# A decoder layer with 16 experts: a quarter of the dense expert moved to the start of the expert loop, the closing additions on one engine

## The chip, the cores and the metric

The kernel runs on one core of a Trainium2 chip. The metric is device time of one execution, in microseconds (us); lower is better. A core has five engines with an instruction queue each: TensorE (PE; its weight loads are counted apart as PEld), VectorE (DVE), ScalarE (ACT), GpSimd (POOL) and SyncE (SP). SP, ACT and POOL also issue DMA transfers here; a row marked SPq or ACTq is such an issue. Each queue runs in its order; the engines wait for each other by semaphores.

## The reference, cut to what matters

`x` is 16 x 64 tokens of 256 values, 1024 tokens in all. After self attention and cross attention comes a mixture of experts with a residual:

```python
scores = softmax(xt @ Wg.T)                      # 16 experts
# the two best of four groups of experts, and in them the four best experts
weights = take_along_axis(scores, topi, axis=1)
h = silu(xt @ W1[e].T) * (xt @ W3[e].T)          # 176 hidden values per expert
y = sum over e of combine[:, e] * (h @ W2[e].T)
z = silu(xt @ Ws1.T) * (xt @ Ws3.T) @ Ws2.T      # shared expert
x = x + y + z
```

## The kernel before, in words

**Work and tiles.** The 1024 tokens are eight tiles of 128 (`NI` = 8), `x[0]` to `x[7]`, which lie two by two in `x_pairs`. Products are made from two float parts of each operand, a rounded high part and the rest: `parts_of` (L111 to L113) rounds on ScalarE (L112) and subtracts on VectorE (L113), and `matmuls` (L102 to L105) sums three products of parts. The attention comes first, up to about 450 us; the experts are the rest.

**Fifteen experts by slots.** For experts 0 to 14 the rows of tokens are sorted into slots: GpSimd scatters them to `xd` in HBM, with 384 slots for each expert. For each expert:

- `expert_weights` loads the weights by SP (L277), ScalarE makes their high part (`w<-w`, L278), and VectorE or GpSimd the low part (L283).
- `expert_inputs` loads the slots' rows (`xr`, by SP), turns them over on TensorE (six transposes, L1265) and makes their parts `xs` (L112, L113).
- `expert_hidden` does the up products (18 matmuls, L104), the silu on ScalarE (`g`, L1283, and `g2`, L1286), the products `h` and `h2` on VectorE (L1284, L1287), and their parts `hp` (L112, L113).
- `send_outputs` does the down products (three blocks of five matmuls, `av<-w,hp`), copies each block to `y` (L1299, ScalarE, or VectorE for one block of most experts), and GpSimd scatters `y` to `yd` in HBM (L1304, three scatters per expert), sorted by choice: a token's four experts are its choices 0 to 3, in the order in which their experts are done.

**The dense expert.** Expert 15 is computed for every token, with a weight that is zero where a token did not choose it; its weights `w_last` are in SBUF from early on. The tokens' first half is done before the loop (`dense_up`, `dense_gated`, `dense_out`). The second half is done in two quarters of 256 tokens: `dense_hidden` (18 up matmuls of 128 columns by 256, `mm<-xn,w_last`, then silu, product and parts) and `dense_output` (two blocks of five matmuls, `av<-w_last,hp`, each followed by `add_last`, L950 to L954, one VectorE addition L952 of the weighted result to `x`).

**The expert loop** (`for e in range(E + 1)`) is staggered: in step `e` the inputs of expert `e` are made, the hidden values of expert `e - 1`, and the outputs of expert `e - 2`. The hidden values of experts 0 and 1 stand at the head of steps 1 and 2. `weights_of_choices(1)`, in step 1, makes the weights of the second half's tokens; its exponential has an ACT table load of its own (L878), and the next silu another (L1283). In the last step the first quarter's hidden values are made (`h_p`).

**The tail.** After the scatters of experts 11 to 14, `load_outputs(k)` reads back choice `k` from `yd` in four transfers of 256 KB (`got<-yd`, L1320, all by SP; nine `got` buffers). `add_outputs(k)` adds them to `x`: two of three tiles by one VectorE instruction (L1334), the third by ScalarE, which scales (L1331), and GpSimd, which adds (L1332). The dense quarters stand between: choice 0, output of the first quarter, choice 1, hidden values and output of the second quarter, choices 2 and 3. Then eight transfers write `out`, by SP and ScalarE in turn (L1392).

**What sets the order.** A scheduler orders each engine's queue by a simulated timeline, bound by what the kernel writes out: inside `with tc.issue_after(i)` nothing is issued before `i`. `up_done[0]` is the last up matmul of the expert done last, `gated[0]` its last part, `silus[-1]` its last silu, `lows[-1]` the last part of the inputs. The tail stands behind the last scatters and `gated[0]`.

Of the kernel before, what the change touches and what calls it, by code (L numbers as in the profile page):

```python
# [29 lines left out]
AF = mybir.ActivationFunctionType  # L30
ALU = mybir.AluOpType
# [11 lines left out]
E, INTER, NGRP, TOPK, TOPKG = 16, 176, 4, 4, 2  # L43
# [28 lines left out]
def decoder_layer(ctx: ExitStack, tc: tile.TileContext, a: dict, out: bass.AP):  # L72
    nc = tc.nc
# [43 lines left out]
    x = [t[:, i, :] for t in x_pairs for i in range(2)]  # L117
# [168 lines left out]
    def expert_up(w, xs, n):  # L286


        ps = [mm_tile(cols=n) for _ in range(3)]
        return ps, [expert_up_part(k, w, xs, t) for k, t in enumerate(ps)][-1]  # L290
# [24 lines left out]
    with ExitStack() as attn:  # L315
# [643 lines left out]
        with (  # L959
# [109 lines left out]
            def dense_weights():  # L1069

                parts = [
                    xw.tile([128, 2, 2, 4 * HQ], F32R, tag=f"w_q{n}", name=f"w_last{n}")
                    .rearrange("p a b c -> p (a b c)")[:, :W_COLS]
                    for n in range(2)
                ]
                up = xb.tile([128, 3, 2, 2, DC], F32, tag="w_s", name="w_last_up")
                down = xb.tile([128, 2, D], F32, tag="w_o0", name="w_last_down")
                for t, cols in (
                    (up.rearrange("p a b c d -> p (a b c d)"), slice(0, W_UP)),
                    (down.rearrange("p a b -> p (a b)"), slice(W_UP, W_COLS)),  # L1080
                ):
                    nc.sync.dma_start(out=t, in_=a["W123"][E - 1][:, cols])
                    parts_of(t, parts[0][:, cols], parts[1][:, cols])
                return parts
# [18 lines left out]
            def dense_gated(g, up, g2, up2):  # L1103
                h_p = [
                    xa.tile([128, 512], F32R, tag=f"roped1{n}", name=f"dense1{n}", bufs=1)
                    for n in range(2)
                ]
                h_p.append(xa.tile([128, 512], F32R, tag="q_r", name="dense2"))
                nc.vector.tensor_tensor(g, up, g, ALU.mult)
                parts_of(g, h_p[0], h_p[1])  # L1110
                nc.vector.tensor_tensor(g2[:64], up2[64:], g2[64:], ALU.mult)
                parts_of(g2[:64], h_p[2][:64], h_p[2][64:])
                return h_p
# [15 lines left out]
            for n in range(len(units) + 2):  # L1129
# [58 lines left out]
                if n == 8:  # L1188
                    w_last = dense_weights()
                    with after(exps[-1]):  # L1190
                        routed.append(weights_of_choices(0))
                if n == 9:
# [30 lines left out]
                    with after(aimed, placed):  # L1223
# [4 lines left out]
                        h_p = dense_gated(*dense_ups)  # L1228
# [9 lines left out]
    gated, up_done = [None], [None]  # L1238
# [34 lines left out]
    def expert_hidden(w, xs, n):  # L1273


        ps, up_done[0] = expert_up(w, xs, n)
        g, h, g2, h2 = (
            fh.tile([128, SLOTS], F32, tag=tag, name=tag)[:, :n] for tag in ("g", "h", "g2", "h2")
        )
        h_p = [  # L1280
            fh.tile([128, SLOTS], F32R, tag=tag, name=tag)[:, :n] for tag in ("hp0", "hp1", "hp2")
        ]
        nc.scalar.activation(g, ps[0], AF.Silu)  # L1283
        nc.vector.tensor_tensor(h, ps[1], g, ALU.mult)  # L1284
        parts_of(h, h_p[0], h_p[1])
        silus.append(nc.scalar.activation(g2[64:], ps[2][:64], AF.Silu).ins)  # L1286
        nc.vector.tensor_tensor(h2[:64], ps[2][64:], g2[64:], ALU.mult)  # L1287
        gated[0] = parts_of(h2[:64], h_p[2][:64], h_p[2][64:])
        return h_p
# [24 lines left out]
    def load_outputs(k):  # L1314

        tiles = []
        for n in range(NI // 2):
            t = fy.tile([128, 2, D], F32, tag="got", name="got", bufs=9)
            first = (E - 1) * SLOTS + (TOPK - 1 - k) * NT + n * 256
            got = nc.sync.dma_start(  # L1320
                out=t, in_=yd[first : first + 256].rearrange("(i p) d -> p i d", p=128)
            ).ins
            behind(got, returned)
            tiles.append(t)
        return tiles

    def add_outputs(k, got, cw):
        for i in range(NI):
            y, w = got[i // 2][:, i % 2], cw[i // 4][:, k, i % 4 : i % 4 + 1]
            if i % 3 == 2:  # L1330
                nc.scalar.activation(y, y, AF.Copy, scale=w)  # L1331
                nc.gpsimd.tensor_tensor(x[i], x[i], y, ALU.add)  # L1332
            else:
                nc.vector.scalar_tensor_tensor(x[i], y, w, x[i], ALU.mult, ALU.add)  # L1334

    def dense_hidden(w, half, n):
        return expert_hidden(w, [p[:, :, n * 256 : n * 256 + 256] for p in normed[half]], 256)

    def dense_output(w, h_p, half, n, add):
        for b in range(2):  # L1340
            ps = av_tile()[:, :D]
            expert_output(ps, w, h_p, slice(b * 128, b * 128 + 128))
            add(half, 2 * n + b, ps)
# [6 lines left out]
    ws, xs, hs, got = {}, {}, {}, {}  # L1350
    with tc.issue_after(lows[-1]), tc.issue_after(silus[-1]):
        ws[0] = expert_weights(a["W123"][0], nc.vector)
    for e in range(E + 1):
        if e in (1, 2):

            low = lows[-1]
            hs[e - 1] = expert_hidden(ws[e - 1], xs[e - 1][0], SLOTS)
        if e < E - 1:
            low = lows[-1]
            with tc.issue_after(up_done[0] if e in (1, 2) else low):  # L1360
                xs[e] = expert_inputs(e)
            if e >= 1:
                with tc.issue_after(low), tc.issue_after(silus[-1]):
                    ws[e] = expert_weights(a["W123"][e], nc.vector if e < 3 else nc.gpsimd)
        if e == 1:
            with tc.issue_after(gated[0]), tc.issue_after(silus[-1]):
                routed.append(weights_of_choices(1))
        if 0 <= e - 1 < E - 1 and e > 2:
            hs[e - 1] = expert_hidden(ws[e - 1], xs[e - 1][0], SLOTS)
        if e - 2 >= 0:  # L1370
            if e == E:

                with tc.issue_after(gated[0]):
                    h_p = dense_hidden(w_last, 1, 0)
            last = send_outputs(e - 2, ws.pop(e - 2), hs.pop(e - 2), xs.pop(e - 2)[1])
            if e - 2 == E - TOPK - 2:
                short = slots_are_short()
            k = e - 2 - (E - 1 - TOPK)
            if k >= 0:
                got[k] = load_outputs(k)  # L1380
    with ExitStack() as behind_last:
        for ins in (*last, gated[0]):
            behind_last.enter_context(tc.issue_after(ins))
        cw = [r[0] for r in routed]
        add_outputs(0, got[0], cw)
        dense_output(w_last, h_p, 1, 0, add_last)
        add_outputs(1, got[1], cw)
        dense_output(w_last, dense_hidden(w_last, 1, 1), 1, 1, add_last)
        for k in range(2, TOPK):
            add_outputs(k, got[k], cw)  # L1390
    for i in range(NI):
        (nc.sync if i % 2 == 0 else nc.scalar).dma_start(  # L1392
# [10 lines left out]
    with tc.If(short > 0):  # L1403
        w_over = [weights_without_slot(half, routed[half][2]) for half in range(2)]
        with tc.For_i(0, E - 1, 1) as e:
            w = expert_weights(a["W123"][bass.ds(e, 1)].rearrange("o p c -> p (o c)"))
# [109 lines left out]
```

## Time and profile before

| | us |
|---|---|
| median of 3 runs | 580.62 |
| the runs | 577.94, 580.62, 586.16 |
| the profiled execution | 577.4 |
| its span, first to last instruction | 575.5 |
| TensorE busy in the span | 540.3 (94%) |
| VectorE busy | 400.2 (70%) |
| ScalarE busy | 279.3 (49%) |
| GpSimd busy | 230.6 (40%) |
| mean granted TensorE clock | 0.978 of full |

All times below are on the clock of the profiled execution, from the start of its span. A row of the timeline reads: start, duration of the group, engine, line and operation, out<-in (buffer numbers left out), shapes and types, the count; in brackets the engine's idle time before it and what ended it. A row of the stretches reads: from and to, length, then busy us (and instructions) of PE, PEld, DVE, ACT and POOL, the granted TensorE clock, the busy share of the DMA engines, and GB/s.

### The profile page before, as it was taken

Reading aid. Unit: us, or ns where it says so; the run is one execution under the profiler, and the core shown is the slowest. Engines: PE = TensorE matmul, PEld = TensorE weight load, DVE = VectorE, ACT = ScalarE, POOL = GpSimd, SP = SyncE. Lnnn points to the kernel's source line nnn. Section 1 sums busy time; section 2 is a strip of 40 time slices with the busy share of each in tenths; the row PEclk is TensorE's granted clock in tenths of the full one; section 3 lists DMA queues with packets and bytes.
Section 4 is the critical chain, followed back from the end, with each engine's and each line's share of the span. In section 5 each row is a group of like instructions: output and inputs, shape, how many; then the busy total and the mean of one; then the engine's idle time right before and its main releaser. Section 6 shows DMA issues by size and latency. Waiting matters only on the chain.

```text
span 575.5 us, 10603 instructions
## 1 busy us (share of the span) xinstructions
PE 540.3 (94%) x4013; PEld 446.7 (78%) x4013; DVE 400.2 (70%) x879; ACT 279.3 (49%) x524; POOL 230.6 (40%) x213
## 2 busy tenths in 40 slices
PE   7999999999999989999999999999999779999962
PEld 5889898888989876757778577685787669999951
DVE  6355566644655788848577586889777479999866
ACT  4677557575574431230432323152525187777551
POOL 4260500101001005426243444632544717888862
PEclk9999999999999999999999999999999789999995
DMA  8564431823200599482020000000511658777384
GB/s 227 145 166 146 111 109 39 227 86 112 75 1 1 167 250 308 111 239 52 2 70 1 8 1 1 0 31 0 188 50 68 202 169 285 240 245 238 122 279 152
DMA packets 56294, 70.83 MB, mean 123 GB/s; under 512 B 13872, under 2 KB 42768, under 8 KB 56240
## 3 DMA queue, kind: packets, MB, share of 16 engines
q1 hardware_dynamic: 51408, 58.71, 34.5%
q0 software_dynamic: 3696, 10.36, 4.7%
q10 hardware_dynamic: 1136, 1.05, 0.6%
q8 instruction: 33, 0.54, 0.4%
q14 instruction: 21, 0.17, 0.1%
HBM read 48.61 MB, written 21.86 MB: 122 GB/s over the span
## 4 chain that ended last, share of the span: by engine, by line
PE 81%; DVE 7%; issue 4%; DMA 3%; ACT 3%; POOL 1%; SPq 1%; DVEq 0%; ACTq 0%; POOLq 0%
PE mm L104 47%; PE mm L1005 7%; PE av L590 5%; PE av L104 5%; PE at L573 4%; PE at L343 3%; PE at L1028 2%; PE av L1041 2%; PE at L1265 2%; PE mm L439 2%; DMA bqkv<-in_bqkv 1%; PE mm L461 1%; DMA got<-yd 1%; DVE x L1334 1%; POOL roped L990 1%
## 5 line engine op out<-in xcount | busy, mean ns | idle before, releaser
L990 POOL TENSOR_TENSOR roped<-rt,rt 128x512 f32<-128x512 f32 x48 | 62.6, 1325 | 83.4 <-DVE rt L984 80.5
L984 DVE TENSOR_TENSOR rt<-mm,rope_q 128x512 f32<-128x512 f32 x96 | 61.4, 685 | 24.3 <-PE mm L104 23.6
L104 PE MATMUL mm<-xn,w_q 128*128 128x512 f32 x288 | 73.9, 403 | 0.5 <-ACT xn L222 0.5
L104 PEld LDWEIGHTS mm<-xn,w_q 128*128 128x128 f32 x288 | 52.2, 188 | 14.0 <-issue 1.8
L104 PE MATMUL mm<-xs,w 128*128 128x384 f32 x270 | 55.3, 354 | 7.0 <-ACT xs L112 5.8
L1304 POOL DMA_INDIRECT yd<-y,to x45 | 47.9, 1064 | 27.6 <-ACT y L1299 13.1
L104 PEld LDWEIGHTS mm<-xs,w 128*128 128x128 f32 x270 | 48.4, 198 | 9.0 <-ACT xs L112 6.6
L327 ACT ACTIVATE p<-p 128x512 f32<-128x512 f32 x32 | 20.1, 629 | 62.3 <-DVE p L326 62.3
L324 DVE TENSOR_REDUCE sm_m<-at 128x8 f32<-128x512 f32 x32 | 21.8, 680 | 37.1 <-PE at L573 36.2
L1005 PE MATMUL mm<-roped,w_s 128*64 128x512 f32 x192 | 46.4, 602 | 0.7 <-POOL roped L990 0.7
L522 POOL TENSOR_TENSOR wv<-code,scale 128x512 fp32r<-128x512 f32 x7 | 9.5, 1360 | 88.2 <-DMA scale<-in_scales 58.7
L613 DVE TENSOR_TENSOR x<-mm,x 128x256 f32<-128x256 f32 x64 | 26.0, 419 | 23.9 <-PE mm L104 21.9
L104 PE MATMUL mm<-wo,o 128*128 128x256 f32 x256 | 39.6, 295 | 0.0
L104 PE MATMUL av<-w,hp 128*128 128x256 f32 x225 | 35.2, 290 | 0.7 <-ACT y L1299 0.7
L104 PE MATMUL mm<-xn,wq 128*128 128x512 f32 x128 | 34.6, 405 | 0.7 <-ACT xn L222 0.5
L104 PE MATMUL mm<-wv,xn 128*128 128x256 f32 x256 | 35.2, 289 | 0.0
L104 PE MATMUL mm<-xn,wk 128*128 128x512 f32 x128 | 34.9, 404 | 0.0
L590 PE MATMUL av<-pt,v 128*128 128x128 f32 x256 | 34.5, 277 | 0.0
L104 PEld LDWEIGHTS mm<-wo,o 128*128 128x128 f32 x256 | 32.9, 190 | 1.5 <-issue 0.4
L590 PEld LDWEIGHTS av<-pt,v 128*128 128x128 f32 x256 | 32.0, 191 | 1.2
L104 PEld LDWEIGHTS mm<-wv,xn 128*128 128x128 f32 x256 | 31.8, 189 | 0.9
L104 PEld LDWEIGHTS av<-w,hp 128*128 128x128 f32 x225 | 30.6, 190 | 1.9 <-ACT y L1299 1.2
(216 smaller groups left out, 1145.8 us busy)
## 6 DMA issues: line engine op xcount, KB each, us to landing
w<-in_W SPq DMA_DIRECT2D x15, 640.0 KB
code<-in_codes SPq DMA_DIRECT2D x32, 256.0 KB
scale<-in_scales SPq DMA_DIRECT2D x32, 256.0 KB
xr<-xd SPq DMA_DIRECT2D x15, 408.0 KB
xd<-zeros SPq DMA_DIRECT2D x8, 720.0 KB
yd<-zeros SPq DMA_DIRECT2D x8, 512.0 KB
got<-yd SPq DMA_DIRECT2D x16, 256.0 KB
wq<-in_Wq SPq DMA_DIRECT2D x4, 512.0 KB
```

The source lines that it names most:

```text
L104: m = nc.tensor.matmul(ps, lhsT=l, rhs=r, start=(n == 0), stop=(n == len(pairs) - 1))
L324: nc.vector.tensor_reduce(m, sc, AX.X, ALU.max)
L327: exps.append(nc.scalar.activation(p, p, AF.Exp, scale=scale).ins)
L343: last = nc.tensor.transpose(ps[:, 2 * n : 2 * n + 2, :].rearrange("p a q -> p (a q)"), pn[:, 2 * n : 2 * n + 2, :].rearrange("p a k -> p ...
L439: nc.tensor.matmul(ps[:, c * DCQ : (c + 1) * DCQ], lhsT=wq[:, h, c * 128 : (c + 1) * 128], rhs=wkq[:, h, :], start=True, stop=True,)
L573: nc.tensor.matmul(sc[par * 64 : par * 64 + 64, 2 * g + pp, :], lhsT=qk[0][:, b * S : (b + 1) * S], rhs=qk[1][:, b * S : (b + 1) * S], sta ...
L590: nc.tensor.matmul(av[:, k * 128 : (k + 1) * 128], lhsT=v[:, i, k0 : k0 + HD], rhs=pt[:, i].rearrange("p a q -> p (a q)"), start=True, sto ...
L613: nc.vector.tensor_tensor(x[i], ps, x[i], ALU.add)
L984: nc.vector.tensor_tensor(mt, ps3, rope_table(t, 2 * ab + k), ALU.mult)
L990: nc.gpsimd.tensor_tensor(r.rearrange("p (b s) -> p b s", s=S), one, two, op)
L1005: nc.tensor.matmul(ps[h // 2][(h % 2) * 64 : (h % 2) * 64 + 64], lhsT=w_s[:, t, blk, ab, :], rhs=roped[2 * t + ab], start=first[h], stop=l ...
L1304: sent = nc.gpsimd.indirect_dma_start(out=yd[: (E - 1) * SLOTS + min(TOPK, E - 1 - e) * NT], out_offset=bass.IndirectOffsetOnAxis(ap=to[:, ...
```

## The change

1. In step 1 of the loop, after the hidden values of expert 0, the hidden values of the dense expert's third quarter of tokens (the second half's first) are made, issued behind expert 0's last up matmul. Its output is made and added in step 2, before the outputs of expert 0 are sent. In the last step only the other quarter is left, and its output stands at the head of the tail.
2. In the tail all additions of the choices' outputs are VectorE instructions.
3. Two of the four loads of the last choice, the odd ones, are issued by ScalarE.

```diff
@@ load_outputs
-            got = nc.sync.dma_start(
+            got = (nc.scalar if k == TOPK - 1 and n % 2 else nc.sync).dma_start(
@@ add_outputs
             y, w = got[i // 2][:, i % 2], cw[i // 4][:, k, i % 4 : i % 4 + 1]
-            if i % 3 == 2:
-                nc.scalar.activation(y, y, AF.Copy, scale=w)
-                nc.gpsimd.tensor_tensor(x[i], x[i], y, ALU.add)
-            else:
-                nc.vector.scalar_tensor_tensor(x[i], y, w, x[i], ALU.mult, ALU.add)
+            nc.vector.scalar_tensor_tensor(x[i], y, w, x[i], ALU.mult, ALU.add)
@@ the loop, e in (1, 2)
             hs[e - 1] = expert_hidden(ws[e - 1], xs[e - 1][0], SLOTS)
+            if e == 1:
+                with tc.issue_after(up_done[0]):
+                    h_p = dense_hidden(w_last, 1, 0)
...
             if e == E:
 
                 with tc.issue_after(gated[0]):
-                    h_p = dense_hidden(w_last, 1, 0)
+                    h_p = dense_hidden(w_last, 1, 1)
+            if e == 2:
+                dense_output(w_last, h_p, 1, 0, add_last)
             last = send_outputs(e - 2, ws.pop(e - 2), hs.pop(e - 2), xs.pop(e - 2)[1])
@@ the tail
-        add_outputs(0, got[0], cw)
-        dense_output(w_last, h_p, 1, 0, add_last)
-        add_outputs(1, got[1], cw)
-        dense_output(w_last, dense_hidden(w_last, 1, 1), 1, 1, add_last)
-        for k in range(2, TOPK):
+        dense_output(w_last, h_p, 1, 1, add_last)
+        for k in range(TOPK):
             add_outputs(k, got[k], cw)
```

In the changed kernel's queues this is where the instructions come to lie: on TensorE the quarter's 18 up matmuls stand directly behind expert 0's 18 and ahead of the six transposes of expert 1; on ScalarE the quarter's `g`, `g2` and both `hp` of expert 0 stand ahead of expert 1's weight copy (L278); the second table load waits for expert 1's first up product; expert 0's down matmuls stand behind the quarter's. From expert 3 up to the last scatters every queue holds the same instructions in the same order as before.

## The prediction

> **What bounds the kernel now.** I read the shares of the page first, then the span cut into stretches, then the rows of each engine in the two zones that the change touches. TensorE is busy for 94% of the span, and it holds 81% of the chain that ended last, VectorE 7%:
>
> ```profile
> PE 540.3 (94%) x4013; PEld 446.7 (78%) x4013; DVE 400.2 (70%) x879; ACT 279.3 (49%) x524; POOL 230.6 (40%) x213
> ...
> PE 81%; DVE 7%; issue 4%; DMA 3%; ACT 3%; POOL 1%; SPq 1%; DVEq 0%; ACTq 0%; POOLq 0%
> ```
>
> An average says nothing of a stage. The stretches (us; busy us and instructions of PE, weight loads, DVE, ACT, POOL; granted clock; DMA share; GB/s) show three:
>
> ```profile
> 460.00:470.00 10.00, 6.68 (x34) 6.45 (x34) 6.98 (x21) 7.49 (x12) 0.96 (x1) 0.83 0.64 220
> 470.00:480.00 10.00, 8.62 (x57) 7.87 (x56) 9.70 (x21) 7.89 (x17) 6.09 (x6) 1.00 0.59 181
> 480.00:490.00 10.00, 10.00 (x74) 10.00 (x73) 9.18 (x17) 8.40 (x18) 6.63 (x7) 1.00 0.83 277
> ...
> 560.00:570.00 10.00, 3.21 (x10) 2.36 (x10) 9.84 (x19) 2.59 (x6) 4.05 (x5) 0.50 0.62 195
> ```
>
> At 460 to 470, the entry of the expert loop, no engine is full: they wait for each other. From 480 to about 550 TensorE is full: what arrives late at 480 stays late. At 560 to 570 VectorE is full and sets the end. The instruction orders of both kernels are the same on every engine from expert 3's stage to the last scatters. So the change is a sum of two terms: the delay with which the loop starts, and what the tail saves.
>
> **The entry: what the early quarter costs.** TensorE, then ScalarE, in the entry:
>
> ```profile
> 454.54 4.82 PE L104 MATMUL mm<-xs,w 128*128 128x384 f32 x18 [1.45 <-ACT xs L112]
> 459.19 0.82 PE L1265 MATMUL at<-ident,xr 128*128 128x128 f32 x6
> 463.24 0.79 PE L104 MATMUL mm<-xs,w 128*128 128x384 f32 x3 [3.23 <-ACT xs L112]
> 463.86 0.62 PE L104 MATMUL av<-w,hp 128*128 128x256 f32 x4
> 464.57 3.25 PE L104 MATMUL mm<-xs,w 128*128 128x384 f32 x9
> ```
>
> ```profile
> 460.57 0.48 ACT L1286 ACTIVATE g<-mm 64x384 f32<-64x384 f32 x1 [1.33 <-PE at L1265]
> 461.08 1.26 ACT L278 CAST w<-w 128x1280 fp32r<-128x1280 f32 x1
> 462.70 0.48 ACT L112 CAST xs<-at 128x384 fp32r<-128x384 f32 x1 [0.37 <-remote]
> ...
> 466.94 1.28 ACT L1283 ACT_TABLE_LOAD   x1
> 468.52 0.49 ACT L1283 ACTIVATE g<-mm 128x384 f32<-128x384 f32 x1 [0.30 <-PE mm L104]
> ```
>
> TensorE has a hole of 3.23 us before 463.24, because ScalarE rounds expert 1's inputs (L112) only at 462.70, behind the weight copy (L278). The order of the changed kernel puts 18 up matmuls of the quarter between expert 0's up matmuls and the transposes of expert 1. Their price is that of the same 18 in the tail, 2.32 us; the ten down matmuls cost two fives, 1.50. The hole covers most of the first: transposes end near 462.4, before the rounding could start.
>
> ScalarE has no such cover. Four instructions now stand between the silu of 460.57 and the weight copy: g and g2 of the quarter (0.40 and 0.38, its rows in the tail) and both hp roundings of expert 0 (0.52 and 0.51), which stood behind the copy before; each waits for a VectorE product in between. 1.8 us of work puts the copy at 462.9 to 463.5. Behind it stand the roundings of expert 1; their low parts on VectorE (L113, now 463.96 and 464.90) wait for the copy's two weight splits (L283, 1.56 us) and for the quarter's four products (h and hp at 0.42, 1.7 us, half of it in VectorE's idle 3.81 and 0.61 us there). So TensorE's nine matmuls of 464.57 start at about 466.7. ScalarE is late with the next step too: the table load of 466.94 now waits for expert 1's first up product, and only then come its 1.28 us and g. I put g at 470.6 (+2.1), the weight split of expert 2 at about +2.4, and TensorE's nine matmuls of expert 2 (473.87 before) at 476.0. The two additions of the quarter (L952, 0.47 each) fall into a VectorE that is 97% busy from 470 to 480; they are part of it. The delay of the loop: **+2.1 us**. Its low end is 1.0 (ScalarE's 1.8 us less the hp work that only moved), its high end 4.5: the quarter's PSUM banks hold expert 0's down matmuls behind VectorE (0.9), and releases by TensorE's semaphores came late here (the rounding at 462.70 started 2.7 us after the transposes' recorded end).
>
> One rule bears on this. The Trainium skill ("TensorE: Matmul & The Clock Gate", the section on the clock gate) has the clock drop to half after an idle window of about 3.4 us and return after a busy one. Here are two windows of that length, the second at half clock:
>
> ```profile
> 461.05:464.47 3.42, 1.23 (x7) 1.05 (x7) 2.63 (x5) 3.01 (x7) 0.15 (x1) 1.00 0.46 156
> 464.47:467.88 3.41, 3.32 (x12) 3.31 (x12) 2.95 (x14) 2.40 (x3) 0.00 (x0) 0.50 0.93 324
> ```
>
> The first was not idle: 1.23 us of matmuls in it, and the clock fell all the same; nine matmuls took 3.25 us instead of the 1.81 at 473.87. With the quarter the first window has about 1.4 us of work. By the rule, no idle window, full clock, 1.4 us back on TensorE, and the delay falls to about 1.2 (ScalarE's chain then holds it). By the row, the window remains cold enough. I take the row: 2.1.
>
> **The tail: what is saved.** VectorE:
>
> ```profile
> 552.59 3.65 DVE L1334 SCALAR_TENSOR_TENSOR x<-got,cw,x 128x256 f32<-128x256 f32 x9
> 558.62 0.85 DVE L1334 SCALAR_TENSOR_TENSOR x<-got,cw,x 128x256 f32<-128x256 f32 x1 [2.38 <-DMA got<-yd]
> ...
> 563.39 1.83 DVE L1334 SCALAR_TENSOR_TENSOR x<-got,cw,x 128x256 f32<-128x256 f32 x2
> 565.25 0.97 DVE L113 TENSOR_TENSOR hp<-h,hp 64x256 fp32r<-64x256 f32 x1
> 566.25 2.15 DVE L1334 SCALAR_TENSOR_TENSOR x<-got,cw,x 128x256 f32<-128x256 f32 x4
> ...
> 569.50 1.66 DVE L1334 SCALAR_TENSOR_TENSOR x<-got,cw,x 128x256 f32<-128x256 f32 x4
> ```
>
> Nine additions in a row take 3.65 us, 0.405 each; beside GpSimd's additions (L1332) single ones take 0.85 to 0.97. From 558.62 to 571.16 VectorE does 15 additions, four add_last and four products of the quarter: 12.5 us, of which 23 x 0.41 = 9.4 are their own and 3.1 are lost to GpSimd.
>
> After: 32 additions and two add_last, 34 x 0.405 = 13.8 us, with GpSimd silent. They can't run through from 552.6, for the loads of choices 1 and 2 land at about 557.9 and 560.95 (the transfers fill the DMA engines there, and that stays). I take the order of the changed queue: 18 instructions lie before the third choice's second tile, and are done by the landing at 560.95; 16 are left, 16 x 0.405 = 6.5, end 567.4; I take 567.6, since the 18 may not quite be done by then. The last choice's four loads landed at 566.05, issued 561.03 to 562.9 by SP:
>
> ```profile
> 561.03 1.90 SPq L1320 DMA_DIRECT2D got<-yd  x4
> ```
>
> Eight additions (3.2 us) after 566.05 would end at 569.3 if all tiles came then; but they land one by one from about 564.6 (ScalarE's scaling of one started then), and only the last pair waits for 566: 566.05 + 0.8 = 566.9 is no later than 567.4. The second queue is where a rule speaks against the change: the Trainium skill ("DMA: Bandwidth & Descriptors", section "Issuing engines are not separate DMA queues") says that several issuers save only issue time. The row gives that as 1.9/4 = 0.48 per load, 0.95 for two; by the rule the landing moves up by at most 0.95, since the DMA engines are full at 563 to 565. ScalarE's queue is empty then, so nothing waits behind the two issues. Worth to the end: 0 to 0.5; I take 0, and allow as much the other way for tiles that now land interleaved. ScalarE loses eight scalings, TensorE 28 matmuls, GpSimd eight additions; off the path, so nothing. Behind VectorE's last instruction come 4.34 us of output transfer, unchanged. Tail: 571.16 - 567.6 = **3.5 us saved**. Low end 2.0: eight additions behind a landing at 566. High end 4.8: VectorE's floor, 552.6 + 13.8 = 566.4, if the last y copies (L1299, which waited 1.75 and 1.12 us on TensorE while the 18 matmuls ran that now are gone) bring the scatters forward by 0.9.
>
> **Sum.** +2.1 - 3.5 = -1.4 us. The profiled execution, 577.4 with a span of 575.5, becomes 576.0 with 574.1. The median of the three runs lies 3.2 above the profiled execution, so 580.6 - 1.4 = 579.2.
>
> **Rivals.**
> (1) *The entry costs more than the tail saves (slower).* The place is ScalarE between 460.57 and the copy. For it: the releases come late, expert 0's down matmuls queue behind add_last, and one more half-clock window is worth up to 1.7 us. Against it: TensorE has the hole. It decides once the delay is over 3.5. At 5.0: +1.5, 582.1.
> (2) *VectorE or the landings bound the tail.* Eight more additions on the engine that is already 98% busy there. For it: eight fewer on two helpers is 3.2 us more on VectorE. Against: it sheds 2 add_last, four products and the 3.1 us of contention. Saved 1.5, delay 2.1: +0.6, 581.2.
> (3) *The entry is hidden.* The hole takes all and the clock stays full: delay 0.8, saved 3.8: -3.0, 577.6.
> (4) *The loop falls into a slower rhythm.* TensorE at 10.00 and VectorE at 9.2 to 9.7 of 10 have little slack; shifted against the loads and scatters, each of 12 experts could lose 1 us: +12, 592. Nothing in the stretches shows it; equal orders speak against it.
>
> **How the numbers follow.** Likeliest 0.50 (576.5 to 581.5 with the spread of runs), (1) 0.18, (2) 0.12, (3) 0.11, (4) 0.09. 2% is 11.6 us, about what a measurement of this kernel can tell from no change; case (4) alone passes it on the slow side: 0.09. No case passes 2% faster (the tail's most is 4.8 us); 0.03 is for the spread of runs, 577.9 to 586.2 before; taken from the rest, 0.88 remains. The range holds all but (4) and the ends: from -4 and 1.5 of spread, 575.0, to +2 and 3, 585.5.
>
> **What would show it.** Right: half clock still at about 464 to 468, the nine matmuls of expert 2 two us later, VectorE's additions at 0.41 to the end, VectorE's last instruction three to four us earlier when counted from the last scatter, TensorE's gap before expert 1 filled by w_last matmuls. Wrong: full clock in the entry; a loop whose stretches are below 9.6 of 10 on TensorE; additions that wait for got at 565 and later; scatters that move by over 1 us against expert 14's matmuls.

## The result, and the profile after

| | before | after |
|---|---|---|
| median, us (12 runs each) | 577.94 | 581.17 |
| range of the runs | 575.88 to 587.99 | 580.05 to 589.09 |
| ratio, 95% interval | | 1.0109 (1.0084 to 1.0134) |
| profiled execution, its span | | 586.48, 584.7 |

The changed kernel is 3.2 us slower in the median, where 1.4 us less was forecast; its time lies inside the range of 575.0 to 585.5, which is wide enough for either sign. Both kernels have some executions about 9 us longer than their others, four of twelve before and five after, and as the ratio of the table leaves out the four and only one of the five it overstates the loss: the medians of the others alone are 576.96 and 580.66, a ratio of 1.006. In the first profile of the changed kernel everything from expert 0 on is some 9 us late, so the times below are read from a second profile of the same kernel (run *again*, span 577.7).

The page of after, its shares of busy time and of the chain:

```profile
PE 536.0 (92%) x4013; PEld 443.2 (76%) x4013; DVE 401.3 (69%) x887; ACT 275.5 (47%) x516; POOL 222.1 (38%) x205
...
PE 81%; DVE 8%; ACT 3%; another core or an unknown queue 3%; issue 2%; DMA 2%; POOL 1%; SPq 0%; DVEq 0%; ACTq 0%
```

TensorE does the same 4013 matmuls and VectorE eight instructions more. The new entry is "an unknown queue 3%": a wait whose end nothing in the trace explains. In this execution it is one ScalarE row, the first rounding for expert 0, and TensorE behind it:

```profile
462.88 0.86 ACT L112 CAST xs<-at 128x384 fp32r<-128x384 f32 x2 [15.37 <-remote]
```

```profile
463.41 5.04 PE L104 MATMUL mm<-xs,w 128*128 128x384 f32 x18 [9.03 <-ACT xs L112]
468.29 2.31 PE L104 MATMUL mm<-xn,w_last 128*128 128x256 f32 x18
```

The transposes that it reads are recorded up to 454.4. Keep the 462.88 in mind; it comes back.

The stretches of *again* (columns as before):

```profile
460.00:470.00 10.00, 7.18 (x38) 6.40 (x38) 7.26 (x24) 5.34 (x11) 0.88 (x1) 0.83 0.63 204
470.00:480.00 10.00, 7.87 (x56) 7.50 (x55) 8.22 (x15) 8.13 (x15) 3.96 (x4) 1.00 0.33 102
480.00:490.00 10.00, 10.00 (x73) 9.96 (x72) 9.48 (x18) 7.62 (x18) 6.80 (x7) 1.00 0.87 277
```

From 480 on TensorE is full, as before. But in the entry it is still idle for 2.8 and 2.1 us of ten, though it was given the quarter's work there. TensorE and ScalarE of *again* in the entry:

```profile
452.85 6.06 PE L104 MATMUL mm<-xs,w 128*128 128x384 f32 x18 [0.99 <-DVE x L952]
458.75 2.31 PE L104 MATMUL mm<-xn,w_last 128*128 128x256 f32 x18
460.90 0.82 PE L1265 MATMUL at<-ident,xr 128*128 128x128 f32 x6
464.53 0.74 PE L104 MATMUL av<-w_last,hp 128*128 128x256 f32 x4 [2.81 <-ACT hp L112]
...
466.75 3.70 PE L104 MATMUL mm<-xs,w 128*128 128x384 f32 x15
...
473.71 0.86 PE L104 MATMUL av<-w,hp 128*128 128x256 f32 x5 [2.13 <-DVE x L952]
```

```profile
460.15 0.50 ACT L112 CAST hp<-h 64x384 fp32r<-64x384 f32 x1
462.52 0.38 ACT L1286 ACTIVATE g<-mm 64x256 f32<-64x256 f32 x1 [1.87 <-PE at L1265]
462.92 1.26 ACT L278 CAST w<-w 128x1280 fp32r<-128x1280 f32 x1
...
469.84 1.28 ACT L1283 ACT_TABLE_LOAD   x1 [1.35 <-PE mm L104]
471.13 0.49 ACT L1283 ACTIVATE g<-mm 128x384 f32<-128x384 f32 x1
```

The quarter's 18 up matmuls (458.75) run without a wait, and after them TensorE has a hole of 2.81 us in the place where the hole of 3.23 was in the profile of before: the hole was not filled, it moved behind the new work.

VectorE in the tail of *again*:

```profile
561.16 5.46 DVE L1330 SCALAR_TENSOR_TENSOR x<-got,cw,x 128x256 f32<-128x256 f32 x13
568.80 4.05 DVE L1330 SCALAR_TENSOR_TENSOR x<-got,cw,x 128x256 f32<-128x256 f32 x10 [2.18 <-DMA got<-yd]
```

The additions run at 0.405 to 0.42 us each, as forecast, but VectorE then waits 2.18 us for the first tile of the last choice, and has ten additions left: the eight of that choice and two of the third, for 22 of the first 24 are done by then.

### The profile page after: what moved, and what is told of

Its sections match the earlier page's. It is cut to its first block, busy times and chain, and to the rows that moved or that the text cites. A ratio compares the mean times of both kernels' runs of the same rounds, so it can differ in the third digit from the quotient of the medians.

```text
span 584.7 us, 10587 instructions
## 1 busy us (share of the span) xinstructions
PE 536.0 (92%) x4013; PEld 443.2 (76%) x4013; DVE 401.3 (69%) x887; ACT 275.5 (47%) x516; POOL 222.1 (38%) x205
## 4 chain that ended last, share of the span: by engine, by line
PE 81%; DVE 8%; ACT 3%; another core or an unknown queue 3%; issue 2%; DMA 2%; POOL 1%; SPq 0%; DVEq 0%; ACTq 0%
PE mm L104 47%; PE mm L1005 6%; PE av L104 6%; PE av L590 5%; PE at L573 4%; PE at L343 3%; PE at L1028 2%; PE av L1041 2%; PE mm L439 2%; PE at L1265 1%; DMA scale<-in_scales 1%; DVE x L1330 1%; PE mm L461 1%; ACT w L278 1%
## 5 line engine op out<-in xcount | busy, mean ns | idle before, releaser
L104 PE MATMUL mm<-xs,w 128*128 128x384 f32 x270 | 53.9, 348 | 10.4 <-ACT xs L112 9.0
```

The costliest lines, as they stand in the source:

```text
L104: m = nc.tensor.matmul(ps, lhsT=l, rhs=r, start=(n == 0), stop=(n == len(pairs) - 1))
```

## The experiments

They ran in five sessions on the chip; in each, kernels are compared with runs of the kernel before of the same session, whose median was 577.63 us in the first, 569.64, 569.85, 572.47 and 569.74 in the others. The theory after the result was that the early quarter costs more in the entry than was forecast, because it delays expert 1's weight copy on ScalarE (A). Rivals: the tail loses what it should save; the loop falls into a slower rhythm; later, that late releases by TensorE (an instruction that waits for a matmul starts long after the record has that matmul end) meet an order of the queues that is worse for them (B).

### Each half of the change alone

*again* is the changed kernel, *before_again* the one before. The other two:

```diff
 early_only: the changed kernel, but
-            nc.vector.scalar_tensor_tensor(x[i], y, w, x[i], ALU.mult, ALU.add)
+            if i % 3 == 2:
+                nc.scalar.activation(y, y, AF.Copy, scale=w)
+                nc.gpsimd.tensor_tensor(x[i], x[i], y, ALU.add)
+            else:
+                nc.vector.scalar_tensor_tensor(x[i], y, w, x[i], ALU.mult, ALU.add)
 and all loads by nc.sync
 tail_only: the kernel before, with the additions and loads of the changed one
```

> The changed kernel once more, for a second trace. In its first trace TensorE's first matmuls of expert 0 start at 463.4 instead of 454.5 us, because the releases of the turned inputs came 8.9 us late; everything behind is shifted by it. Theory A (the entry costs more than was forecast): without that stall the nine matmuls of expert 2 still come 4 to 5 us later than 473.9, and the tail saves about 1; the time is 3 to 5 us above the kernel before. Theory B (the tail saves nothing, the landings of the last choice set the end): the entry costs 1.3 us as in the first trace, and VectorE's last instruction comes 14 us or more after the last scatter's issue, with a wait for got near the end; the time is 2 to 5 us above. Theory C (the stall itself is what the change brings): the stall is in this trace too.

> The early quarter alone: the choices' outputs are added as before, every third by ScalarE and GpSimd, and all loads are SP's. Theory A: the time is that of the changed kernel to within 1.5 us, 3 to 5 us above before; the entry rows are the same as in the changed kernel. Theory B (VectorE's own additions or the second queue make the tail late): 1 to 3 us faster than the changed kernel, since GpSimd takes eight additions off a tail that VectorE ends. Theory C: the stall in the entry, 4 us or more above before.

> The tail alone: all additions on VectorE and the second queue, the quarter at the end as before. VectorE then has 40 instructions at 0.41 in the tail instead of 32 of which six are slowed: 31 of them from 558.6, so it ends at about 571.3, as before. Theory A: within 1 us of before. Theory B: 2 us or more slower than before, as the eight additions come on top. Theory C: as before, no stall.

> The kernel before once more, for a second trace, to see how steady the entry is from run to run. Theories A and B: the first matmuls of expert 0 start at 454 to 455 us, or some 9 us later in a disturbed run; the rest follows them rigidly, with 19.3 us from there to the nine matmuls of expert 2. Theory C: never a stall here.

| | median | ratio (95%) | first up product of expert 0 to last scatter | last scatter to VectorE's end |
|---|---|---|---|---|
| before_again | 576.72 (one run) | | 101.65 | 14.58 |
| tail_only | 577.99 | 1.0020 (0.9993 to 1.0046) | 101.60 | 14.25 |
| early_only | 582.85 (580.86 to 583.08 without the two of 587.40 and 589.40) | 1.0127 (1.0077 to 1.0176) | 105.58 | 13.45 |
| again | 580.31 | 1.0053 (1.0034 to 1.0073) | 105.85 | 14.15 |

The early quarter alone makes the whole loss, 3.9 to 4.2 us between expert 0's first up product and the last scatter, with or without the new tail. The new tail alone changes nothing. (In early_only GpSimd's last addition ends after VectorE's: counted from the last scatter to the end of the span, the four tails are 19.22, 19.05, 19.66 and 19.00 us.) The loop itself is rigid: from the seven up matmuls in expert 3's step (at 478.26 in before_again, 481.12 in again) to the last scatter it takes 77.38 us in before_again, 77.58 in again, 77.34 in early_only and 77.42 in tail_only. So no rhythm changed, and the 4 us are in the entry. There, one stretch from expert 0's first up product to those seven matmuls, before_again and then again:

```profile
453.99:478.26 24.27, 19.57 (x102) 18.35 (x102) 17.83 (x43) 15.16 (x27) 10.45 (x10) 0.84 0.68 218
```

```profile
452.85:481.12 28.27, 23.32 (x130) 21.74 (x130) 19.53 (x48) 16.28 (x30) 11.29 (x11) 0.84 0.57 188
```

The reader should subtract: 28 matmuls more (the quarter's 18 and 10) and 3.75 us more of busy TensorE, at the same granted clock of 0.84; the rest of the stretch, in which TensorE does nothing, is 4.70 us in one and 4.95 in the other. early_only gives 28.24, 23.13 busy, 5.11 idle; tail_only 24.18, 19.48 and 4.70. The quarter's matmuls come on top of the idle time, whole: their forecast price was 2.32 and 1.50.

The pair of profiles that the result came with shows less. There the stretch is 24.99 us in after, 21.01 busy at clock 0.93, against 23.72 and 19.02 at 0.86 in before, and from the first up product to the last scatter after takes 102.56 us against 101.46: 1.1 more. In after the late wait lies ahead of the first up product, and none lies inside the stretch.

### The delay on ScalarE, taken away

```diff
 silu0: expert 1's weights are issued behind expert 0's silu, as before the change
             if e == 1:
+                silu, gate = silus[-1], gated[0]
                 with tc.issue_after(up_done[0]):
                     h_p = dense_hidden(w_last, 1, 0)
+                silus.append(silu)
```

```diff
 table_early: the silu's table is loaded right behind the exponential
+            if half == 1:
+                one = fs.tile([128, 1], F32, tag="one", name="one")
+                with tc.issue_after(exps[-1]):
+                    nc.scalar.activation(one, m[:, :1], AF.Silu)
```

The values of `gate` and `one` are used nowhere. *both_early* has both edits. *silu0b*, *silu0c* and *both_early2* repeat kernels, *again2*, *again3* and *before2* are the two kernels themselves. *one_queue* is the changed kernel with all loads by SP.

In session 2:

> The changed kernel, but expert 1's weights are issued behind expert 0's last silu again, and not behind the quarter's: only ScalarE's copy of expert 1's weights (L278) moves forward, to ahead of the quarter's two silus. Theory A, now stated closer: the weight copy stands behind the quarter's last silu and so behind TensorE's last up matmul of the quarter and its late release; it starts 10.1 us after expert 0's first up matmul instead of 5.9 to 6.5. Then here it starts at about 6.5, and the steady loop (the seven matmuls of expert 3's step, 478.3 in before) comes 1 to 2 us after before's instead of 4.0 to 4.5, counted from expert 0's first up matmul; the time is 2 to 3 us below the changed kernel. Theory A2 (the second table load, which waits for expert 1's first up product, sets it): the copy moves, g does not, under 1 us gained. Theory A3 (TensorE's place itself, 18 matmuls ahead of the transposes): under 1 us gained.

> The changed kernel with one silu of one column directly behind the exponential of the second half's weights, so that the table load for the silus (1.28 us) no longer waits for expert 1's first up product. The result of that silu is used nowhere. Theory A2: expert 1's g comes 1.3 us earlier and the time falls by 1.3. Theory A (the weight copy): the load moves off the path, but g still waits for expert 1's up matmuls, which are late by the copy; 1.0 to 1.3 us of the 4 are this load's, the rest stays. A3: nothing.

Measured: 570.00 and 569.68 us, both level with before's 569.64. That looked like a full answer for either edit, but the changed kernel itself had not run in that session. So in session 3:

> The changed kernel beside its variants on one chip. The four runs before were on another chip, where the releases in the entry are not late (last_split has the weight copy 6.8 us after expert 0's first up matmul, not 10.1) and both kernels take 8 us less. Theory A on a chip with late releases: 3 to 4 us above before, weight copy at 10, last scatter 105.5 to 106 us after the first up matmul. On a chip without: 1.5 to 2.5 us above before, copy at 6.8, last scatter at about 102. Rival (the cost is the same on every chip and has nothing to do with the releases): 3 us above on either.

> The kernel before, for its trace on the same chip. With late releases: weight copy 5.8 to 6.5 us after expert 0's first up matmul, last scatter 101.5 after it. Without: copy at 4.5 to 5.5, last scatter at 99.5 to 101; VectorE's last addition 13.5 to 15 us after the last scatter's issue on either.

> Both repairs of the entry together: expert 1's weights behind expert 0's last silu, and the one-column silu behind the exponential (used nowhere). Theory A: the copy at about 6 and g no longer behind the load: last scatter 100.5 to 102 us after the first up matmul; 1 to 3 us below the changed kernel, and up to 1.5 below before, as the tail's gain is then left. If the end of the tail is set by transfers that do not start earlier: no more than the better of the two single repairs.

> The first repair once more (only the weight copy moves), beside the changed kernel on one chip. Theory A with late releases: the copy at 6 to 6.5 instead of 10.1, the last scatter 2 to 4 us earlier counted from the first up matmul, the time 2 to 3 us below the changed kernel. Without late releases: 1.5 below it, as before. A2 (table load): under 1 us.

Measured: the changed kernel loses only 1.2 us in session 3 (571.07 against 569.85), both_early nothing (569.80), silu0b 0.8 (570.63); before2 took 569.61. In session 4:

> The changed kernel beside its repairs, in the hope of a chip with late releases in the entry, where it was 3.1 us above before (again); on the two chips without them it was 1.2 above (again2). With late releases: weight copy 10 us after expert 0's first up matmul, last scatter 105.5 to 106 after it, time 3 to 4 us above before. Without: 6.6 to 6.8, 101.5 to 103, and 0.5 to 2 us above.

> Only the weight copy moved ahead of the quarter's silus. Theory A with late releases: the copy at 6 to 6.5, the last scatter at 102 to 104, the time 2 to 3 us below the changed kernel beside it. If the late releases themselves hold TensorE's next matmuls wherever the copy stands: under 1 us below it. Without late releases: within 0.7 us of it, as in silu0b.

> Both repairs (the weight copy, and the one-column silu whose result is used nowhere). Theory A with late releases: 2.5 to 4 us below the changed kernel, level with before. Without: 0.5 to 1 below the changed kernel, as in both_early.

> The changed kernel with all loads on SP: what the second queue is worth. The forecast was 0 to 0.5 us: the last choice's four loads are then issued in 1.9 us instead of 1.0, and the last tile lands up to 0.95 later; VectorE has ten additions to do from the first tile's landing and takes a tile's two in 0.81, so a tile may land every 0.8 us without making it wait: 0 to 0.3 us slower. Rival: the queues share what limits them, and the second one gains nothing or loses: 0 or faster.

Measured: 578.93, 578.28, 576.25 and 579.79 us, all slower than before's 572.47.

The stretch is that of the table above, cut by the same two landmarks (us; idle is its length less TensorE's busy time); the copy is ScalarE's for expert 1, counted from expert 0's first up product:

| session: kernel | median, less before | ratio (95%) | copy at | stretch | busy | idle | clock |
|---|---|---|---|---|---|---|---|
| 2: silu0 | +0.4 | 1.0002 (0.9991 to 1.0013) | 4.66 | 25.40 | 21.47 | 3.93 | 0.93 |
| 2: table_early | +0.0 | 1.0001 (0.9992 to 1.0010) | 6.82 | 24.46 | 21.43 | 3.03 | 0.93 |
| 3: before2 | -0.2 (one run) | | 4.76 | 22.44 | 18.19 | 4.25 | 0.92 |
| 3: again2 | +1.2 | 1.0018 (1.0010 to 1.0026) | 6.61 | 23.96 | 19.65 | 4.31 | 1.00 |
| 3: both_early | -0.05 | 1.0008 (0.9997 to 1.0019) | 4.73 | 23.98 | 19.97 | 4.01 | 1.00 |
| 3: silu0b | +0.8 | 1.0018 (1.0006 to 1.0029) | 4.74 | 25.52 | 21.42 | 4.10 | 0.93 |
| 4: again3 | +6.5 | 1.0103 (1.0073 to 1.0132) | 11.30 | 30.39 | 22.03 | 8.36 | 0.83 |
| 4: silu0c | +5.8 | 1.0093 (1.0062 to 1.0124) | 5.55 | 28.79 | 23.12 | 5.67 | 0.82 |
| 4: both_early2 | +3.8 | 1.0058 (1.0041 to 1.0076) | 4.66 | 27.79 | 21.54 | 6.25 | 0.88 |
| 4: one_queue | +7.3 | 1.0116 (1.0087 to 1.0144) | 10.66 | 29.04 | 21.01 | 8.03 | 0.88 |

Three things follow. First, A falls as the main cause: silu0c moves the copy forward by 5.8 us against again3 and has 2.7 us less idle time in the stretch, but is only 0.65 us faster in the median, and 5.8 us of loss remain; silu0b is 0.4 below again2, with the same ratio. In session 2 the one kernel with the unmoved entry is last_split (below), 2.0 above before; but from the first up product to the last scatter it takes 101.86 us, between table_early's 101.60 and silu0's 102.79, so its loss does not speak for A. With the early table beside it (both_early2) 2.0 us more come off in session 4, but in the trace that is a shorter busy time at a higher clock (21.54 us at 0.88 against 23.12 at 0.82) and no less idle time (6.25 against 5.67), so the gain can't be put down to the table. Second, the idle part of the stretch is 4.3 to 5.1 us with the quarter in sessions 1 and 3 and 4.2 to 4.7 without it; with the early table or the early copy it is 3.0 to 4.1 in sessions 2 and 3. Third, the price of the same change ranges from +1.2 to +6.5 us between sessions. In session 3 the profiled again2 had the full clock throughout, before2 had not; that pays back part of the quarter. It is also the fastest of that kernel's 22 executions (568.99, where the median is 571.07), so it shows the change near its best. The two stretches, before2 and again2:

```profile
448.43:470.87 22.44, 18.19 (x101) 16.11 (x102) 17.25 (x45) 14.83 (x27) 12.61 (x12) 0.92 0.75 250
```

```profile
448.60:472.56 23.96, 19.65 (x129) 18.15 (x130) 19.34 (x47) 16.13 (x30) 12.63 (x12) 1.00 0.70 226
```

In session 4 the idle part of the changed kernel is 3.4 to 4.1 us larger than in again and again2; of the kernel before there is no trace in that session. ScalarE and TensorE of again3 show where:

```profile
457.62 0.50 ACT L112 CAST hp<-h 64x384 fp32r<-64x384 f32 x1
462.37 0.38 ACT L1286 ACTIVATE g<-mm 64x256 f32<-64x256 f32 x1 [4.25 <-remote]
462.77 1.26 ACT L278 CAST w<-w 128x1280 fp32r<-128x1280 f32 x1
```

```profile
455.43 2.31 PE L104 MATMUL mm<-xn,w_last 128*128 128x256 f32 x18
457.59 0.82 PE L1265 MATMUL at<-ident,xr 128*128 128x128 f32 x6
464.39 1.22 PE L104 MATMUL av<-w_last,hp 128*128 128x256 f32 x4 [5.99 <-ACT hp L112]
```

The quarter's second silu (g2) reads products that are recorded as done at 457.7, and starts at 462.37. Moving the copy ahead of it, in silu0c, leaves that silu where it is, and expert 1's roundings behind it:

```profile
457.69 1.26 ACT L278 CAST w<-w 128x1280 fp32r<-128x1280 f32 x1
...
462.45 0.38 ACT L1286 ACTIVATE g<-mm 64x256 f32<-64x256 f32 x1 [2.41 <-remote]
462.85 0.86 ACT L112 CAST xs<-at 128x384 fp32r<-128x384 f32 x2
```

In both_early2 it starts at 462.32, after a wait of 3.53. In again2, of a session without such waits, the same instruction:

```profile
454.81 0.38 ACT L1286 ACTIVATE g<-mm 64x256 f32<-64x256 f32 x1 [0.45 <-PE mm L104]
```

### The order of the queues, and the last choice

If B holds, it should help to put expert 1's inputs ahead of the quarter on TensorE and ScalarE:

```diff
 quarter_later (and quarter_later2)
-            if e == 1:
-                with tc.issue_after(up_done[0]):
-                    h_p = dense_hidden(w_last, 1, 0)
...
+        if e == 1:
+            with tc.issue_after(lows[-1]):
+                h_p = dense_hidden(w_last, 1, 0)
```

```diff
 last_split: two of the last choice's eight additions by ScalarE and GpSimd again
+            if k == TOPK - 1 and i % 3 == 2:
+                nc.scalar.activation(y, y, AF.Copy, scale=w)
+                nc.gpsimd.tensor_tensor(x[i], x[i], y, ALU.add)
+            else:
+                nc.vector.scalar_tensor_tensor(x[i], y, w, x[i], ALU.mult, ALU.add)
```

> The early quarter issued behind expert 1's inputs and weights instead of ahead of them, the tail as in the changed kernel. The scheduler then also places the exponential and the down matmuls otherwise. Theory A: most of the entry's cost goes, 2 to 4 us below the changed kernel, at or up to 1 us below before. A3: as well, since the transposes no longer stand behind the 18 matmuls; only silu0 tells these two apart. If it stays at the changed kernel's time, the entry has no room for a quarter in any place, whatever the order.

> The changed kernel, but of the last choice's eight additions two are done by ScalarE and GpSimd as before. The tail theory: the last choice's four tiles land 10 to 12 us after the last scatter's issue and VectorE then still has ten additions, 4.1 us, to do. With eight left, VectorE ends 0.8 us earlier, if GpSimd's two additions do not slow it; the time falls by 0.5 to 0.8, within the spread. If VectorE's additions take 0.85 or more beside GpSimd's, it is as slow as the changed kernel.

> The quarter's hidden values stand behind expert 1's input roundings on ScalarE and behind its transposes on TensorE; the rest as in the changed kernel. Theory (what stands ahead of expert 1's roundings when TensorE's releases come late is the cause): level with before, within 1.5 us, in a session with late releases (a wait of over 1.5 us on TensorE near 462 after work that had long ended) as in one without (there +1.0 was measured). Rival (any early quarter costs its own work, wherever it stands in the entry): +3 to +6.5 us with late releases, like the unmoved one. Rival (the additions' and loads' part costs it): the entry no longer than before's 101.5 from expert 0's first up product to the last scatter, and the tail after it longer than 15 us. If no late release shows, only the first number can be compared, and the cause stays open.

> The kernel before, for a trace of the same session: with late releases the second rounding of expert 1's inputs waits until about 462.7 and the loop's last scatter lies 101.5 us after expert 0's first up product; without, 99.7.

quarter_later: 570.64, 1.0016 (1.0005 to 1.0027) in session 2; again, in session 5: 571.01, 1.0027 (1.0017 to 1.0038), with 101.93 us from the first up product to the last scatter against 100.37 in before3, and 13.59 us from there to VectorE's end against 14.75. No late release appeared in either session, so B is not decided. Nor did the order become quite what was wanted: in quarter_later2 six of the quarter's 18 up matmuls run at 449.37, ahead of 15 of expert 0's, and the other twelve behind expert 1's transposes; on ScalarE the quarter's g stands ahead of expert 1's weight copy and only its g2 behind the roundings. In this order the quarter still costs 1.6 us in the entry, hardly less than the 1.85 of again2 against before2. last_split: 571.62, 1.0045 (1.0029 to 1.0062), no help. one_queue, in the table above, is 0.9 us slower than again3 in the median, inside the spread of both (577.89 to 580.11 and its own): the second queue is worth 0 to 0.9, no more than the 0.95 of issue time that the prediction allowed it.

No version was faster than before. table_early, silu0, both_early and tail_only are level with it.

## Why the prediction was wrong

Two terms of the sum failed. Forecast were +2.1 for the entry and -3.5 for the tail; session 1 has +4.2 and -0.4 (again against before_again). So 2.1 us were missed in the entry and 3.1 in the tail.

**The entry, TensorE's part: the first step that failed.** "The hole covers most of the first", the prediction said of the quarter's 18 up matmuls, and put the cost on ScalarE's chain alone (+2.1). Measured: +3.9 to +4.2 in session 1; in the stretch to expert 3's step, again against before_again, 3.75 us of TensorE work and 0.25 of idle time. A hole covers work only if what ends the hole does not wait for that work. Here it does: expert 1's copy and roundings stand on ScalarE behind the quarter's g2, and that silu waits for the quarter's matmuls. The chain of work that ended last shows it in again2 (start, us, what; pieces between these are left out, here and in the next rows):

```profile
449.75 5.04 PE mm L104 x33
454.81 0.38 ACT g L1286
455.21 1.27 ACT w L278
456.50 1.56 DVE w L283 x2
458.42 0.57 DVE xs L113
459.04 2.87 PE mm L104 x15
```

The 33 matmuls are fifteen of expert 0 and the quarter's 18. In before2 the same chain leaves TensorE after the fifteen, and the copy starts at 453.19. Expert 1's transposes, which also stand behind the 18, are in neither chain. Moving the copy ahead of g2 opens another way: in silu0b the chain runs over VectorE, where the quarter's products h stand ahead of expert 1's low parts.

```profile
453.64 1.27 ACT w L278
457.00 0.42 DVE h L1284
458.04 0.43 DVE h L1287
458.50 0.57 DVE xs L113
459.11 2.88 PE mm L104 x15
```

Counted from expert 0's first up product, these fifteen matmuls start at 10.21 us in silu0b and at 10.44 in again2: the copy alone was worth 0.2. In again all 36 matmuls are in the chain, and behind them the late start of g2 at 462.52.

**The second hole.** The prediction counted the quarter's two additions (L952) as part of a busy VectorE. They carry a wait: the down matmuls of expert 0 need the PSUM banks that they empty. VectorE of again:

```profile
471.66 0.56 DVE L1284 TENSOR_TENSOR h<-mm,g 128x384 f32<-128x384 f32 x1 [1.97 <-ACT g L1283]
472.13 0.41 DVE L893 TENSOR_TENSOR ch<-ch,kept 128x256 f32<-128x256 f32 x1
472.58 0.56 DVE L1287 TENSOR_TENSOR h<-mm,g 64x384 f32<-64x384 f32 x1
473.17 0.48 DVE L952 SCALAR_TENSOR_TENSOR x<-av,cl,x 128x256 f32<-128x256 f32 x1
```

L952 stands behind expert 1's product h, which waits for ScalarE's table load of 469.84 and its silu; TensorE's 2.13 us before 473.71 are that chain. In again2 the wait is 2.11. With the table early it is 0.83 in table_early and 0.95 in both_early2, but 2.15 in both_early, so the table load is only a part of it. Before the change another wait stood here; TensorE of before_again:

```profile
461.59 0.80 PE L104 MATMUL mm<-xs,w 128*128 128x384 f32 x3 [1.58 <-issue]
...
469.76 0.80 PE L104 MATMUL mm<-xs,w 128*128 128x384 f32 x3 [2.12 <-ACT xs L112]
```

The prediction had the bank wait only in its high end, at 0.9.

**The entry, ScalarE's part: mechanism right, too small where releases come late.** The four instructions stand ahead of the copy as forecast, and the copy comes 1.85 us later in again2 than in before2 (forecast 1.8 to 2.4). In session 1 it is 10.06 us after the first up product instead of 5.91, for the late release adds to it. The forecast +2.1 fits session 3, without late releases: the matmuls behind expert 1's low parts start 2.2 us later (459.04 less 448.60, against 456.69 less 448.43), by the copy, splits and products that were forecast, and the last scatter comes 1.85 later (101.57 against 99.72 from the first up product). The fit of the whole entry is luck in part, for again2 had the full clock: silu0b, traced near its median at clock 0.93, takes 102.67.

**The clock: undecided.** Row and rule were weighed for the window ahead of expert 1's up products, and half clock taken. Two successive stretches of again, and of again2 in the same place:

```profile
462.00:465.00 3.00, 0.47 (x4) 0.47 (x4) 2.19 (x4) 2.46 (x5) 0.00 (x0) 1.00 0.25 71
465.00:468.00 3.00, 3.00 (x12) 2.45 (x11) 2.91 (x10) 1.82 (x3) 0.00 (x0) 0.53 0.62 211
```

```profile
456.00:459.00 3.00, 1.77 (x9) 1.24 (x9) 2.47 (x5) 2.98 (x6) 1.98 (x2) 1.00 0.39 122
459.00:462.00 3.00, 2.96 (x18) 2.87 (x19) 2.81 (x15) 1.09 (x3) 0.00 (x0) 1.00 0.57 177
```

With 0.47 us of matmuls in three, half clock followed (15 matmuls in 3.70 us); with 1.77, full clock (2.87 us for the same 15). The rule cited in the prediction, a drop after an idle window, fits these two; but the 1.23 us of work before the drop in the profile of before shows that idle need not be empty, and in table_early the 3.41 us before the drop at 459.44 held 2.00 us of matmuls, more than the 1.77 after which again2 kept the full clock. How much work prevents the drop, these runs don't say. Each of the two came, from trace to trace: in session 2 silu0 and table_early took 4.44 us for the 15 matmuls, at half clock for most of it, and last_split had the full clock. The clock is worth up to 1.6 us and the profile of before could not tell it. It did not make session 1's loss: 0.84 in both stretches, and a busy time that grew by the quarter's own price.

**The tail: the second step that failed; mechanism right, size wrong.** Contention with GpSimd is gone. But of 3.5 us saved, counted from the last scatter to VectorE's end, there came 0.4 in session 1 (14.58 to 14.15), 1.1 in the profiles of before and after (15.16 to 14.02), 1.2 in quarter_later2, which has the same tail (14.75 to 13.59), and 2.6 in session 3 (14.91 to 12.31). The failed term is "only the last pair waits for 566". Ten additions wait for the last choice's first tile: 4.05 us behind a landing 10.1 us after the last scatter in again, 8.2 in again2. The faster VectorE only reaches that landing sooner and idles 2.18 us. The loads of the last choice also go out later, 5.27 us after the last scatter against 3.90 in before_again: in all traces with the early quarter 4.6 to 6.7, in those without 3.5 to 3.9 and, in before, 5.0. In again SP waits ahead of them for the last scatter's landing in `yd`; why that comes later, no run shows. In sum for session 1: the first up product 1.14 earlier (it varies between executions of both kernels, 452.9 to 454.7), +4.20 to the last scatter, -0.43 in the tail, +0.17 behind it: 2.8, the difference of the spans (577.7 and 574.9).

**The rivals.** (1), the entry costs more than the tail saves, is what happened; its price of 5.0 for the entry and +1.5 in all was nearer than the likeliest case, and it named the late releases and the PSUM banks. Its odds of 0.18 were too low. (2) holds for the tail beside it; that its 581.2 is the measured median is luck, for it took the entry at 2.1. (3) is excluded by the entry, and (4) by the rigid 77.3 to 77.6 us.

**What stays open.** Why the same change costs 1.2 us in one session and 6.5 in another is only half explained: the extra idle time lies behind a release that comes late, and the early quarter puts a silu that waits for it ahead of expert 1's roundings. Whether roundings placed first would escape it, no run shows.

## What to carry to other kernels

A hole on the bounding engine is room for new work only if the instruction that ends the hole does not depend on what the new work delays; follow the wait back through every queue before you count it as cover, and otherwise charge the new work in full. Cut the stretch around an edit by two landmarks that both kernels share, and compare busy and idle time: one subtraction told here what no list of waits did. In a tail, count how many instructions are left when the last transfers land: speed before that landing only lengthens the wait for it, unless it also brings the landing forward.

## What the runs showed that was not expected

Releases by TensorE come late in some sessions. In the first, in the profile after and in the fourth, instructions that wait for TensorE resume at 462.3 to 463.0 us whatever kernel runs and whenever TensorE's record ends: 462.70 in before, 462.89 in before_again (work recorded as done at 460.0), 462.88 in tail_only, 462.52 in again, 462.37, 462.45 and 462.32 in again3, silu0c and both_early2 (done at 457.7, 459.3 and 457.7), 462.88 in after (454.4). That is 1.5 to 8.5 us. In sessions 2, 3 and 5 no such wait shows. In all of these traces GpSimd sends its `xd` scatters (L842) until 460.5 to 461.4, shortly before the waits end, and in again2, before2, silu0, table_early, before3 and quarter_later2, of sessions without late releases, only until 458.0 to 458.5; whether the scatters hold the releases was not tried, and the recorded ends of matmuls are modelled, so the cause is open.

The sessions differ before the entry too: expert 0's first up product comes at 448.4 to 449.1 us in the second, third and fifth, at 451.4 to 452.1 in the fourth, and at 452.9 to 454.7 in the first. The second and the fourth have the same chip number on record, 14, and only the fourth has late releases; if that is one chip, the chip is not the cause.
